# Layer 3's dense first block: the weights' relu on ACT, the addition and the mask in one DVE operation per head

## The chip, the cores and the metric

The kernel runs on one core of a Trainium2 chip. The metric is the device time of one execution in microseconds. The kernel before takes 1708.3 us, the median of three runs (1705.78 to 1711.26).

A core has five engines that run their own instruction queues in order: PE (matrix products), DVE (elementwise work and reductions), ACT (activations), POOL (here above all the issue of gathers) and SP (here the issue of plain loads and stores). They wait for each other through semaphores.

## The reference

Four graph layers run over 3327 nodes with 512 features and a sparse random adjacency `adj`, whose low-numbered nodes have many more edges than the others. After each layer the input is added and the rows are normalised. Only layer 3 is touched, a graph attention layer with four heads of 128 outputs:

```python
h = jnp.einsum('nf,hfo->hno', x, hamilton)
f_src = jnp.einsum('hno,ho->hn', h, a_src)
f_dst = jnp.einsum('hno,ho->hn', h, a_dst)
e = jax.nn.leaky_relu(f_src[:, :, None] + f_dst[:, None, :], ALPHA)
e = jnp.where((adj > 0)[None, :, :], e, NEG_INF)
attn = jax.nn.softmax(e, axis=-1)
h_prime = jnp.einsum('hnm,hmo->hno', attn, h)
out = jnp.transpose(h_prime, (1, 0, 2)).reshape(N, -1)
return jax.nn.elu(out)
```

## The kernel before

The nodes are cut into 26 blocks of 128 (the last has 127). Layer 3 first writes a table `t_d` to memory, one row per node, with the projected features of the four heads and their scores (520 floats a row). The sums over neighbours are then made in two ways.

**Blocks 1 to 25** use lists of edges. POOL gathers 128 table rows at a time (a chunk, L966) into a ring of 27 slots (22 in `gt`, 5 in `gx`). Groups of up to four chunks go through six stages, one stage per iteration of the main loop (`Gat.group`): 1, the gathers, and `far` on ACT (L1156); 2, `ds` on DVE (L1160); 3, small products `pg` on PE (L1168); 4, `sc` on DVE (L1178, L1179), two exponentials and `sel` on ACT (L1180, L1181, L1185); 5, the gathered rows times their weights on DVE (L1188); 6, the sums `acc` on PE (L1196), which give the ring's slots back.

**Block 0**, the heaviest, is done densely (`Gat.first_block`). Exponentials are factored so that the weight of neighbour j for node i and head h is `max(f1[i]*up[j], low[j])` times the 0/1 mask. `f1` is broadcast over the partitions once (`f1b`, L1102); `up` and `low` are made in `Gat.factors`. Each of the 26 blocks of neighbours is a unit (`unit(c)`):

- stage 1: SP loads 128 table rows into `gd` (L1119; four buffers, so unit c's load waits for the matmuls of unit c-4; for unit 25 it is 127 rows);
- stage 2: every fourth unit, ACT converts the mask of four units to `mk` (L1124; one buffer). DVE makes `wt` (two buffers), four L1128, one per head, and multiplies it with the mask, one L1130. ACT writes ones into a column of `gd` (L1131), for which the load must have landed;
- stage 3: PE adds the four heads' products to block 0's sums (L1134).

The order of all instructions on each engine is as the program writes them here; no scheduler moves them. `steps(n)` starts a unit and moves every live unit on by one stage, n times: 12 times before the first group, then twice in each iteration, ahead of the groups' stages. So in each iteration two units pass each stage, and then each live group does one of its own, older groups first. In the kernel before, PE's order from group 1's sums on is: unit 20, unit 21, group 1's sums, products of group 4, units 22 and 23, group 2's sums, products of group 5, unit 24, unit 25, group 3's sums, products of group 6, group 4's sums.

A block's end (`summed`, then L825) runs on ACT and DVE when its sums are complete.

Of the kernel before, what the change touches and what calls it, by code (L numbers as in the profile page):

```python
# [8 lines left out]
F32 = mybir.dt.float32  # L9
# [8 lines left out]
AF = mybir.ActivationFunctionType  # L18
ALU = mybir.AluOpType
# [4 lines left out]
P = 128  # L24
BIG = 1e30
EPS = 1e-5
GAT_ALPHA = 0.2
# [548 lines left out]
class Ring:  # L576
# [19 lines left out]
    def done(self):  # L596

        self.live.pop(0)
# [23 lines left out]
def sparse_path(ctx, tc, flag_i, x, adj, l0_w, l0_a1, l0_a2, l1_w_self, l1_b_self, l1_w_nb, l1_b_nb,  # L622
# [13 lines left out]
    nc = tc.nc  # L636
    N, D = x.shape
    NB = (N + P - 1) // P
# [10 lines left out]
    def pool_in(lay, name, bufs=1, **kw):  # L649
        return lay.enter_context(tc.tile_pool(name=name, bufs=bufs, reuse_waits="tile", **kw))  # L650
# [3 lines left out]
    keep = pool_in(ctx, "s_keep")  # L654
# [328 lines left out]
    class Gat:  # L983
        def __init__(self, name, table, H, OUT, w, k):
            self.table, self.H, self.OUT, self.w, self.k = table, H, OUT, w, k
            self.M = OUT + 2
            self.fall = keep.tile([P, 3 * H, NB], F32, name=name + "fall")
            self.own = keep.tile([P, 3, 2 * H, NB], BF16, name=name + "own")
            self.xsum = keep.tile([P, DC, NB], F32, name=name + "xsum")
            self.up, self.low = [keep.tile([P, H, NB], F32, name=name + x) for x in ("up", "low")] if k else (None,) * 2  # L990

        def products(self, ps, xt):

# [76 lines left out]
        def factors(self, pool, bc, f2):  # L1070

            H = self.H
            far = pool.tile([P, H], F32, name="farz")
            nc.vector.tensor_add(far, bc[:, :H], bc[:, 2 * H:3 * H])
            most = pool.tile([P, 4], F32, name="most")
            nc.vector.tensor_reduce(most[:, 0:1], far, AX.X, ALU.max)
            nc.vector.tensor_reduce(most[:, 1:3], bc[:, :2 * H].rearrange("p (s h) -> p s h", s=2), AX.X, ALU.max)
            nc.vector.tensor_reduce(most[:, 3:4], bc[:, 2 * H:], AX.X, ALU.max)  # L1080
            nc.vector.tensor_scalar(most[:, 0:1], most[:, 0:1], 0.0, 1.0 - GAT_ALPHA, ALU.max, ALU.mult)
            nc.vector.scalar_tensor_tensor(most[:, 0:1], most[:, 1:2], GAT_ALPHA, most[:, 0:1], ALU.mult, ALU.add)
            nc.vector.tensor_scalar(self.up, f2, most[:, 0:1], None, ALU.subtract)
            nc.vector.tensor_scalar(self.low, f2, GAT_ALPHA, most[:, 0:1], ALU.mult, ALU.subtract)
            for t in (self.up, self.low):
                nc.scalar.activation(t, t, AF.Exp)
            wide = pool.tile([P, 1], F32, name="wide")
            nc.vector.scalar_tensor_tensor(wide, most[:, 2:3], GAT_ALPHA, most[:, 0:1], ALU.mult, ALU.add)
            nc.vector.scalar_tensor_tensor(wide, most[:, 3:4], 1.0 - GAT_ALPHA, wide, ALU.mult, ALU.add)
            return wide  # L1090

        def first_block(self, pool, ps, pacc, mp, none, done):

            H, OUT, M = self.H, self.OUT, self.M
            hh = H // 2
            dg = pool.tile([P, H, P], F32, name="wt")
            for h in range(H):
                nc.vector.tensor_scalar(dg[:, h, :], ident, self.fall[:, h, 0:1], None, ALU.mult)
            pf = ps.tile([P, H * P], F32, name="pf", tag="pg")
            nc.tensor.matmul(pf, ones, dg.rearrange("p h i -> p (h i)"), start=True, stop=True)  # L1100
            f1 = pool.tile([P, H, P], F32, name="f1b", bufs=1)
            nc.scalar.activation(f1, pf.rearrange("p (h i) -> p h i", i=P), AF.Exp, scale=1.0 - GAT_ALPHA)  # L1102

            pl = ps.tile([P, H * P], F32, name="pl", tag="pg")
            nc.tensor.matmul(pl[0:1, :P], none, ident, start=True, stop=True)
            lone = pool.tile([P, H, P], F32, name="wt")[0:1, 0, :]
            nc.scalar.copy(lone, pl[0:1, :P])
            G = pool.tile([P, H, M], F32, name="gd", bufs=4)
            nc.sync.dma_start(G[0:1].rearrange("p h m -> p (h m)"), self.table[0:1, :])
            nc.scalar.copy(G[0:1, :, OUT], ones[0:1, :H])  # L1110
            acc = [pacc.tile([P, hh, M], F32, name="acc") for s in range(2)]
            for s in range(2):
                nc.tensor.matmul(acc[s], lone, G[0:1, s * hh:(s + 1) * hh, :], start=True, stop=False)
            masks = [None]

            def unit(c):
                m = LAST if c == NB - 1 else P
                G = pool.tile([P, H, M], F32, name="gd", bufs=4)
                nc.sync.dma_start(G[:m].rearrange("p h m -> p (h m)"), self.table[2 + c * P:2 + c * P + m, :])  # L1119
                yield  # L1120
                if c % 4 == 0:
                    masks[0] = mp.tile([P, 4, P], F32, name="mk")
                    n = min(4, NB - c)
                    nc.scalar.activation(masks[0][:, :n, :], row0[:, c:c + n, :], AF.Identity)  # L1124
                mask = masks[0]
                wt = pool.tile([P, H, P], F32, name="wt")
                for h in range(H):
                    nc.vector.tensor_scalar(wt[:m, h, :], f1[:m, h, :], self.up[:m, h, c:c + 1],  # L1128
                                            self.low[:m, h, c:c + 1], ALU.mult, ALU.max)
                nc.vector.tensor_mul(wt[:m], wt[:m], mask[:m, c % 4, None, :].to_broadcast([m, H, P]))  # L1130
                nc.scalar.copy(G[:m, :, OUT], ones[:m, :H])  # L1131
                yield
                for h in range(H):
                    nc.tensor.matmul(acc[h // hh][:, h % hh, :OUT + 1], wt[:m, h, :], G[:m, h, :OUT + 1],  # L1134
                                     start=False, stop=h % hh == hh - 1 and c == NB - 1)
                if c == NB - 1:
                    done(0, acc)

            for c in range(NB):
                yield unit(c)  # L1140
# [607 lines left out]
```

## Time and profile before

| what | value |
|---|---|
| median of three runs | 1708.3 us (1705.78 to 1711.26) |
| profiled execution, first to last instruction (span) | 1704.1 us |
| median less that span | 4.2 us |
| busy in the span: PE, DVE, POOL, ACT | 1523.7, 1243.4, 911.9, 773.2 us |
| four L1128 and one L1130, in the dense block | 28.2 + 17.2 us busy for 25 of 26 units |
| first L1128, last L1134 | 1381.6, 1449.5 us |

The page gives for the profiled execution the span from its first to its last instruction; a run's time is a few microseconds longer. Times inside the span count from its start. In the timeline and the chain the columns are start, duration, engine and line; a bracket gives the idle time before the instruction and what ended it. A matmul in fp32 is two instructions, so a unit's four heads appear as eight.

### The profile page before, as it was taken

Reading aid. Unit: us, or ns where it says so; the run is one execution under the profiler, and the core shown is the slowest. Engines: PE = TensorE matmul, PEld = TensorE weight load, DVE = VectorE, ACT = ScalarE, POOL = GpSimd, SP = SyncE. Lnnn points to the kernel's source line nnn. Section 1 sums busy time; section 2 is a strip of 40 time slices with the busy share of each in tenths; the row PEclk is TensorE's granted clock in tenths of the full one; section 3 lists DMA queues with packets and bytes.
Section 4 is the critical chain, followed back from the end, with each engine's and each line's share of the span. In section 5 each row is a group of like instructions: output and inputs, shape, how many; then the busy total and the mean of one; then the engine's idle time right before and its main releaser. Section 6 shows DMA issues by size and latency. Waiting matters only on the chain.

```text
span 1704.1 us, 25362 instructions
## 1 busy us (share of the span) xinstructions
PE 1523.7 (89%) x7947; PEld 981.5 (58%) x7947; DVE 1243.4 (73%) x3256; ACT 773.2 (45%) x2411; POOL 911.9 (54%) x1008
## 2 busy tenths in 40 slices
PE   5798958999999999999999999889989866998774
PEld 4565746777666664444444444446555545877653
DVE  8999988999998973124777884565434468798986
ACT  6557855667776764111111121122223222566664
POOL 2000067777666613646776552477777552677770
PEclk9999979999999999999999999999999987999997
DMA  8623687998775637978998776589999664677772
GB/s 300 233 100 107 207 288 237 313 309 266 258 231 176 179 90 282 317 237 272 341 328 296 246 241 241 204 279 317 318 312 322 234 227 157 189 230 224 227 220 74
DMA packets 121982, 410.17 MB, mean 241 GB/s; under 512 B 24768, under 2 KB 26304, under 8 KB 121838
## 3 DMA queue, kind: packets, MB, share of 16 engines
q0 software_dynamic: 69584, 286.13, 52.8%
q1 hardware_dynamic: 52254, 122.32, 20.4%
q8 instruction: 65, 1.06, 0.3%
q14 instruction: 79, 0.65, 0.1%
HBM read 360.34 MB, written 48.04 MB: 240 GB/s over the span
## 4 chain that ended last, share of the span: by engine, by line
PE 61%; DVE 16%; DMA 11%; ACT 6%; issue 3%; POOL 2%; SPq 0%; DVEq 0%; ACTq 0%; POOLq 0%
PE po L765 20%; PE acc L1196 15%; PE acc L1474 14%; DMA gt<-t_d,idx 7%; PE po L998 6%; PE pt L750 2%; DVE cand L877 2%; DVE gt L1188 2%; DMA gx<-t_d,idx 2%; POOL gt L966 2%; PE pg L1168 2%; DMA gd<-t_d 1%; DVE cand L891 1%; DVE sl L889 1%; ACT h L1213 1%
## 5 line engine op out<-in xcount | busy, mean ns | idle before, releaser
L966 POOL DMA_INDIRECT gt<-t_d,idx x739 | 742.1, 1004 | 578.9 <-DVE some L893 210.6
L1196 PE MATMUL acc<-gt,sel 128*128 128x264 f32 (+4 forms) x1656 | 413.7, 399 | 27.1 <-issue 20.1
L1196 PEld LDWEIGHTS acc<-gt,sel 128*128 128x128 f32 (+2 forms) x1656 | 311.4, 195 | 97.8 <-issue 42.9
L1188 DVE TENSOR_TENSOR gt<-gt,pg 128x1536 f32<-128x1536 f32 (+2 forms) x128 | 238.6, 1864 | 6.3 <-ACT gt L1181 2.9
L765 PE MATMUL po<-wn,xt 128*128 128x512 f32 x416 | 192.9, 607 | 3.8 <-ACT xt L753 3.8
L1474 PE MATMUL acc<-gt,sall 128*128 128x512 bf16 x489 | 117.3, 379 | 17.6 <-DMA gt<-t_d,idx 14.3
L765 PEld LDWEIGHTS po<-wn,xt 128*128 128x128 f32 x416 | 77.2, 193 | 89.4 <-issue 78.4
L966 POOL DMA_INDIRECT gx<-t_d,idx x107 | 107.6, 1006 | 38.6 <-issue 14.9
L877 DVE MAX8 cand<-val 128x8 f32<-128x832 uint16 (+38 forms) x259 | 125.7, 522 | 0.0
L1474 PEld LDWEIGHTS <-sall 128*128 128x128 fp8e4 x603 | 58.3, 97 | 98.4 <-issue 35.3
L1474 PE MATMUL acc<-gt,sel 128*128 128x512 bf16 (+3 forms) x486 | 113.3, 379 | 0.0
L998 PE MATMUL po<-gt,xt 128*128 128x268 f32 x416 | 106.0, 400 | 2.0 <-ACT xt L757 1.7
L1474 PEld LDWEIGHTS <-sel 128*128 128x128 bf16 (+3 forms) x603 | 57.9, 98 | 80.0 <-issue 22.7
L1156 ACT ACTIVATE far<-place,nmid 128x384 int16<-128x384 int16 (+3 forms) x137 | 86.9, 637 | 37.5 <-DVE ds L1160 34.5
L753 ACT COPY xt<-pt 128x512 f32<-128x512 f32 x86 | 50.8, 591 | 113.3 <-PE pt L750 113.2
L998 PE MATMUL po<-w,xt 128*128 128x262 f32 x416 | 96.2, 384 | 1.6 <-ACT xt L757 1.6
L765 PE MATMUL po<-wl,xt 128*128 128x512 f32 x208 | 94.0, 594 | 2.9 <-ACT xt L753 2.9
L765 PE MATMUL po<-wx,xt 128*128 128x512 f32 x208 | 94.3, 596 | 1.3 <-ACT xt L753 1.2
L750 PE MATMUL pt<-s_ident,xres 128*128 128x128 f32 x520 | 79.9, 277 | 17.4 <-DMA xres<-in_x_dram 16.6
L750 PEld LDWEIGHTS pt<-s_ident,xres 128*128 128x128 f32 x520 | 63.8, 143 | 46.2 <-issue 31.2
L1009 ACT COPY tg<-po 128x264 f32<-128x264 f32 (+1 forms) x104 | 39.9, 392 | 110.8 <-PE po L998 108.9
L849 ACT ACTIVATE m<-ab 128x1664 bf16<-128x1664 int32 x50 | 80.4, 1607 | 20.5 <-DMA ab<-in_adj_dram 15.6
(273 smaller groups left out, 2555.4 us busy)
## 6 DMA issues: line engine op xcount, KB each, us to landing
ab<-in_adj_dram SPq DMA_DIRECT2D x25, 832.0 KB
ab<-in_adj_dram SPq DMA_DIRECT2D x25, 831.5 KB
t_d<-t SPq DMA_DIRECT2D x50, 384.0 KB
gt<-t_d POOLq DMA_DIRECT2D x38, 384.0 KB, 7.8
gt<-t_d,idx POOLq DMA_INDIRECT x739, 4.8
t_d<-tg SPq DMA_DIRECT2D x25, 264.0 KB
t_d<-tg SPq DMA_DIRECT2D x25, 260.0 KB
gd<-t_d SPq DMA_DIRECT2D x25, 260.0 KB
```

What stands on the lines that cost most here:

```text
L750: nc.tensor.transpose(pt[:, c, :], src[:, c * P:(c + 1) * P], ident)
L753: nc.scalar.copy(xt, pt)
L765: nc.tensor.matmul(po, xt[:, c, :], w[:, c], start=c == 0, stop=c == DC - 1)
L849: nc.scalar.activation(m, ab[s], AF.Sign, accum_out=half[:, s, b:b + 1])
L877: nc.vector.max(out=top, in_=seg)
L966: nc.gpsimd.indirect_dma_start(out=t[:m, c, :], out_offset=None, in_=table[:, :], in_offset=bass.IndirectOffsetOnAxis(ap=l.idx[:m, c0 + c: ...
L998: nc.tensor.matmul(pw[s], xt[:, c, :], self.w[:, c, s, :], start=c == 0, stop=c == DC - 1)
L1009: nc.scalar.copy(tb[:, s * hh:(s + 1) * hh, :], by_head[:, :, 1:])
L1156: nc.scalar.activation(far[:, :g * P], place[:, c0 * P:(c0 + g) * P], AF.Abs, bias=l.nmid, scale=2.0)
L1188: nc.vector.tensor_mul(Gc[:, :, :OUT], Gc[:, :, :OUT], w[:, :g].rearrange("p c (h o) -> p (c h) o", o=1).to_broadcast([P, g * H, OUT]))
L1196: nc.tensor.matmul(accs[b][s], S[:m, c, :], G[:m, c, s * hh * M:(s + 1) * hh * M], start=at + c == 0, stop=at + c == chunks_of[b] - 1)
L1474: nc.tensor.matmul(accs[b], S[:m, c, :], G[:m, c, k * D:(k + 1) * D], start=at + c + k == 0, stop=k == 2 and at + c == n - 1)
```

## The change

`low` is kept negated (`nlow`), by one more DVE operation in `factors`. Per head, ACT computes `relu(f1*up + nlow)`; a stage later, DVE computes `(that - nlow) * mask` in one operation per head. The result is the same, since `max(a, b) = relu(a - b) + b`. The unit has four stages rather than three: load; `mk` and relu; DVE's operations and the ones copy; matmuls.

```diff
-            self.up, self.low = [keep.tile([P, H, NB], F32, name=name + x) for x in ("up", "low")] if k else (None,) * 2
+            self.up, self.nlow = [keep.tile([P, H, NB], F32, name=name + x) for x in ("up", "nlow")] if k else (None,) * 2
...
-            nc.vector.tensor_scalar(self.low, f2, GAT_ALPHA, most[:, 0:1], ALU.mult, ALU.subtract)
-            for t in (self.up, self.low):
+            nc.vector.tensor_scalar(self.nlow, f2, GAT_ALPHA, most[:, 0:1], ALU.mult, ALU.subtract)
+            for t in (self.up, self.nlow):
                 nc.scalar.activation(t, t, AF.Exp)
+            nc.vector.tensor_scalar(self.nlow, self.nlow, -1.0, None, ALU.mult)
...
                 for h in range(H):
-                    nc.vector.tensor_scalar(wt[:m, h, :], f1[:m, h, :], self.up[:m, h, c:c + 1],
-                                            self.low[:m, h, c:c + 1], ALU.mult, ALU.max)
-                nc.vector.tensor_mul(wt[:m], wt[:m], mask[:m, c % 4, None, :].to_broadcast([m, H, P]))
+                    nc.scalar.activation(wt[:m, h, :], f1[:m, h, :], AF.Relu, bias=self.nlow[:m, h, c:c + 1],
+                                         scale=self.up[:m, h, c:c + 1])
+                yield
+                for h in range(H):
+                    nc.vector.scalar_tensor_tensor(wt[:m, h, :], wt[:m, h, :], self.nlow[:m, h, c:c + 1],
+                                                   mask[:m, c % 4, :], ALU.subtract, ALU.mult)
                 nc.scalar.copy(G[:m, :, OUT], ones[:m, :H])
                 yield
```

In PE's order each unit's matmuls move back by one unit: unit 19, unit 20, group 1's sums, products of group 4, units 21 and 22, group 2's sums, products of group 5, units 23 and 24, group 3's sums, products of group 6, unit 25, group 4's sums. On ACT, the relu of unit c+1 stands behind the ones copy of unit c. The other engines' orders are otherwise unchanged.

## The prediction

> **What bounds the kernel now.** I read the page first, then the chain that ended last in order of time around the changed lines (1376 to 1460 us), then POOL's instructions one by one, then the groups by shape for prices. The chain, from the stretch of layer 3's dense block:
>
> ```profile
> 1404.23 1.12 DVE wt L1128 x4
> 1405.45 0.69 DVE wt L1130
> ...
> 1426.57 0.61 ACT far L1156
> 1427.32 2.10 PE acc L1134 x8
> 1429.47 18.04 DMA gd<-t_d
> 1447.85 2.09 PE acc L1134 x8
> 1449.93 5.49 PE acc L1196 x16
> ...
> 1455.64 3.60 PE acc L1196 x16
> ```
>
> To 1422 the chain runs on DVE: four L1128 and one L1130 per unit, 1.75 us from one unit to the next. Then it changes. Unit 21's matmuls (1427.32) free the buffer that unit 25's load needs; that load takes 18.04 us, unit 25's matmuls wait for it, and only behind them on PE stand group 3's sums (L1196, 1449.93) and group 4's (1455.64). The last load, not DVE, is what the chain holds here.
>
> POOL's instructions say what this costs at the end:
>
> ```profile
> 1431.89 0.95 POOL L966 DMA_INDIRECT gt<-t_d,idx  x1 [22.90 <-ACT pg L1180]
> ...
> 1452.41 0.96 POOL L966 DMA_INDIRECT gt<-t_d,idx  x1 [9.47 <-issue]
> ...
> 1457.47 0.95 POOL L966 DMA_INDIRECT gt<-t_d,idx  x1 [0.30 <-issue]
> ...
> 1665.51 0.94 POOL L966 DMA_INDIRECT gt<-t_d,idx  x1 [0.30 <-issue]
> ```
>
> POOL fills the ring by 1409 and stands 22.90 us until group 1's sums give slots back, then 9.47 us until group 3's do. From 1452.41 to its last gather at 1665.51 no gap exceeds 0.31 us: one gather each 1.26 us, 38 us before the end. So the end moves with the time at which POOL becomes free for good. A microsecond of DVE saved in the dense block is worth something only if it brings that forward.
>
> Prices of the operations (groups by shape: busy us, mean ns of one):
>
> ```profile
> L1128 DVE TENSOR_SCALAR wt<-f1b,g3up,g3low 128x128 f32<-128x128 f32 x100 | 28.2, 355 | 6.5 <-PE acc L1134 3.2 <-ACT f1b L1102 2.9 <-PE acc L1113 0.4
> L1130 DVE TENSOR_TENSOR wt<-wt,mk 128x512 f32<-128x512 f32 x25 | 17.2, 688 | 1.3
> ...
> L1213 ACT ACTIVATE h<-acc,rden 128x128 f32<-128x128 f32 x104 | 29.0, 357 | 0.0
> L825 ACT ACTIVATE o<-e,nm,rs 128x512 f32<-128x512 f32 x26 | 20.8, 801 | 2.8 <-DVE nm L824 2.8
> L1218 DVE SCALAR_TENSOR_TENSOR h<-h,xres 128x512 f32<-128x512 f32 x26 | 18.0, 691 | 12.7 <-ACT e L1216 12.5
> L1216 ACT ACTIVATE e<-h 128x512 f32<-128x512 f32 x26 | 16.4, 630 | 0.8
> ```
>
> L825 has two per-partition operands (bias and scale) as the new relu has; L1216 has none, and at the same shape is 0.17 us shorter. L1213 has one, at the relu's own shape.
>
> [...]630 ns without, 801 with two, and the chain shows L825 as 0.71, which is 0.09 less.[...]L1218's 691 ns beside L1130's 688 says it costs like a two-tensor one.[...]unit 25's, the only one with 127 rows, takes 18.04 us, the 128-row ones 3.3 to 6.3 from issue to their ACT copy.
>
> **The change, part by part.**
>
> *Removed from DVE:* per unit 4 L1128 and one L1130, 1.75 us.
>
> *Added to DVE:* per unit four scalar_tensor_tensor of 128x128. [...]From one to the next about 0.21 (neighbours on this engine overlap by 0.08, as L1130 does), up to 0.29. Four: 0.84 to 1.16 us, so DVE is relieved by 0.6 to 0.9 us a unit. It can't use it: each of the four waits for its head's relu.
>
> *Added to ACT:* per unit four relus. [...]from one to the next 0.48 - 0.09 = 0.39; four occupy 1.56 us. Bounds: 0.26 each if they went like L1213 (one operand, four in 1.03 to 1.12), 0.48 without overlap. I take 0.39. With the ones copy (0.10) and a quarter of mk (0.53, plus some 0.3 in which it now waits for DVE's reading of the old mk), a unit is 1.56 + 0.10 + 0.2 = 1.86 us of ACT. That is as long as DVE's 1.75 was. And ACT also has, in each pair of units from group 1 on, far (0.62), two exponentials (0.24) and sel (0.53). ACT takes over as the pacing engine.
>
> *New waits on ACT.* The ones copy of unit c waits for its load, and relu c+1 is queued behind it; formerly DVE worked ahead there. Behind relu stand far, the exponentials and sel of the groups. In turn relu c waits for unit c-2's matmuls (two wt buffers). The last ones copy still stands in front of group 5's exponentials, as before.
>
> *The extra DVE negation in the factors:* it waits for ACT's second Exp (ends 1374.56; DVE's next operation started 1374.15) and takes 0.2: DVE's chain to L1098, PE's broadcast and f1b all shift by 0.65 us. No cover: PE waits 6.22 us there for DVE.
>
> *Moved:* a unit has one stage more, so its matmuls come a half iteration later in program order: PE does units 0 to 20 before group 1's sums (formerly 0 to 21), and unit 21 comes after them and after group 4's small products; unit 25 comes after group 3's sums and before group 4's. SP's loads keep their order, but unit 25's load still waits for unit 21, now behind group 1.
>
> *The sum.* ACT from its first relu at 1382.9 (1381.52 + 0.65 for f1b, mk 0.6) to unit 20's ones copy: 21 x 1.56 = 32.8 for relu, 21 x 0.10 = 2.1 for ones, 5 x 0.8 = 4.0 for mk with its wait, 5 far 3.1, two groups' exponentials and sel 1.5, zero copies 0.3: 43.8, so 1426.7. ACT also waits, for loads in the stretch where the gathers keep the DMA engines full and about 2 us for group 2's scores, which stand behind the 2.28 us L1188 on DVE: 1429. Unit 20's matmuls at half clock, 2.1: group 1's sums start about 1431.7, against 1429.20: **+2.5**.
> Unit 21 then ends after those sums (5.7 at half clock, as before), the products (0.5) and its own 1.1: 1439.0, against 1429.44 (+9.5). The load lands 18.04 later, 1457.0; ones 0.2 and unit 25 at half clock 2.1[...]: group 4's sums start at 1459.3 against 1455.64. That is 9.5 less the 5.7 of group 3's sums and products, which no longer stand between: **+3.7**.
> POOL: in the kernel before, the first slot came back 2.5 us after group 3's sums began (1449.93 to 1452.41, half clock) and 1.3 after group 2's (1436.94 to 1438.25, full clock). The gather at 1457.47 becomes 1459.3 + 1.3 to 2.5 = 1460.6 to 1461.8: +3.1 to +4.3. It is the thirteenth after the ring filled, in both; from there POOL is saturated.
> The profiled span becomes 1704.1 + 4 = 1708.1. The median of the runs lies 4.2 above that span, and I let that offset stand: 1708.3 + 4 = **1712.3 us**.
>
> **Rivals.**
> - *ACT follows the rate of L1213* (0.26 from relu to relu). 21 x 4 x 0.13 = 11 us less ACT work, of which the waits for loads and for wt give back most; group 1's sums start about 1.6 us before 1429.20. By the sum above group 4's sums are then level with before (-4.1 + 3.7), and if PE also keeps full clock through units 20, 21 and group 1 (1.0 + 1.0 + 2.1), up to 4.5 us earlier, 6 with the first slot's release. For it: four L1213 in 1.03. Against it: L825's 801 ns. 1702 to 1708.5; say 1706.
> - *Slower by more than 0.3%: relu to relu 0.48, or PE's half clock lasts longer.* Place: from group 1's sums to group 4's. PE was at half clock for unit 21 (2.10 rather than 1.13) and group 1 (5.72 rather than 3.6) behind a 2.9 us pause; the change makes the pauses before unit 20 as long and the one before unit 25 some 7 us (6.0 before). If every PE step between 1428 and 1462 is at half clock, unit 21 and 22 add 1, group 2's and 3's sums delay nothing, group 4's add 2. With no overlap on ACT, 21 x 4 x 0.09 = 7.6 us are added directly. It decides once group 1's sums start 4 us late or more (1433.2). 1714 to 1718; say 1716.
> - *The shift is absorbed:* POOL's saturation, or the 38 us of tail on ACT and DVE, has slack. Speaks against it: no POOL gap over 0.31 in 213 us, and the chain at the end leaves POOL only at 1665.51, for that gather's landing. 1708.3.
> - *The change doesn't do what it says:* no; relu(f1*up - low) + low is max(f1*up, low), DVE does lose the 4+1 operations, only the time isn't worth what it looks like.
>
> **How the numbers follow.** +4 case 0.46 (range 1709 to 1714.5); slower rival 0.36; fast ACT 0.12; absorbed 0.06. 0.3% is 5.1 us, about what a measurement of this kernel tells from no change (the three runs span 5.5): the +4 case lies inside it, save a sixth of it. Slower: 0.36 less 0.02, plus 0.08 = 0.42. Faster, that is below 1703.2: a third of the fast-ACT case, 0.04. The rest, 0.54, is within. Range: 1705 leaves out the fastest end, 1718 the worst half-clock and no-overlap ends.
>
> **What the profile after would show.** Right: relus of 0.48 us and 0.39 apart; DVE idle on ACT between its four operations; units 1.9 to 2.1 us apart; group 1's sums near 1431.7; group 3's sums ahead of unit 25; unit 25's load issued near 1439 and 18 us long; POOL's final run from a gather near 1461. Wrong: relus 0.26 apart and group 1 before 1429 (first rival), group 1 after 1433 (second), or POOL's last gather later but the end not (third). If POOL has further gaps after 1462, the step from group 4 to the end fails.

## The result and the profile after

The changed kernel takes 1712.89 us (median of 20 runs, 1707.96 to 1715.24); the kernel before took 1708.53 us beside it (20 runs, 1705.19 to 1714.2). The ratio is 1.0023, 95% interval [1.0015, 1.0031]: 4.4 us slower, by less than 0.3% save for the upper end of the interval. The predicted 1712.3 us lies 0.6 us from it.

The chain that ended last in the kernel after, in order of time (start, duration, what):

```profile
1394.40 1.63 ACT wt L1129 x4
...
1416.43 1.56 ACT wt L1129 x4
...
1425.88 1.56 ACT wt L1129 x4
...
1427.72 2.28 DVE gt L1192
...
1430.66 0.60 issue
...
1432.42 2.09 PE acc L1138 x8
1434.51 4.24 PE acc L1200 x16
...
1439.05 1.00 PE acc L1138 x8
...
1440.11 18.77 DMA gd<-t_d
...
1459.20 2.09 PE acc L1138 x8
1461.28 4.50 PE acc L1200 x16
```

Where the chain of before ran through DVE's four L1128 and one L1130 it now runs through ACT's relus. From the first relu (1386.20) to unit 20's ones copy (1432.19) ACT stands idle for 2.9 us in all: it has become the pacing engine. The end of the stretch has the same shape as before with its parts exchanged: unit 20's matmuls (1432.42), group 1's sums (1434.51), only then unit 21 (1439.05), whose end lets unit 25's load start (1440.11); that load is 18.77 us long, and behind unit 25 stand group 4's sums (1461.28).

POOL's instructions in the kernel after where it had to wait, with the idle time before each in the bracket:

```profile
1436.86 1.02 POOL L966 DMA_INDIRECT gt<-t_d,idx  x1 [24.49 <-DVE sc L1183]
...
1442.56 0.95 POOL L966 DMA_INDIRECT gt<-t_d,idx  x1 [0.90 <-ACT mk L1125]
...
1449.08 0.97 POOL L966 DMA_INDIRECT gt<-t_d,idx  x1 [1.83 <-issue]
...
1463.76 0.95 POOL L966 DMA_INDIRECT gt<-t_d,idx  x1 [9.94 <-ACT far L1160]
...
1672.27 0.92 POOL L966 DMA_INDIRECT gt<-t_d,idx  x1 [0.30 <-issue]
```

The two long stands (POOL waiting for a free slot of the ring) are still there, 24.49 us (22.90 before) and 9.94 us (9.47). The engine named in a bracket is inferred and need not be the one that frees a slot: the long stands end 2.35 and 2.48 us after the start of the sums on PE that give slots back, group 1's (1434.51) and group 4's (1461.28). After 1463.76 no gap between gathers is longer than 0.31 us, and the last gather starts at 1672.27.

The groups by shape (busy us, mean ns of one, idle time before it and what ended it), kernel after:

```profile
L1129 ACT ACTIVATE wt<-f1b,g3nlow,g3up 128x128 f32<-128x128 f32 x100 | 41.0, 481 | 3.4 <-PE acc L1138 3.2
L1133 DVE SCALAR_TENSOR_TENSOR wt<-wt,g3nlow,mk 128x128 f32<-128x128 f32 x100 | 33.6, 346 | 19.2 <-ACT wt L1129 16.2
```

A relu takes 481 ns, and four in a row 1.63 us, so 0.38 to 0.39 from one to the next. DVE waits 16.2 us for relus in this block.

Times of two executions can't be set side by side as they stand. The two profiled executions differ ahead of the change, as the small matmul `pb` (L1043) shows, up to which both execute the same work. Its start before, and then after:

```profile
1372.23 0.39 PE L1043 MATMUL pb<-dgm,s_ones 16*128 16x16 f32 x2 [0.63 <-DVE dgm L1041]
```

```profile
1375.62 0.39 PE L1043 MATMUL pb<-dgm,s_ones 16*128 16x16 f32 x2 [0.63 <-DVE dgm L1041]
```

Those 3.39 us aren't the change's: in the profiles of e1 to e4 below, `pb` starts anywhere from 1370.62 to 1376.20. So from here on positions are counted from `pb`:

| from `pb`, us | before | after | difference |
|---|---|---|---|
| group 1's sums start | 56.97 | 58.68 | +1.7 |
| unit 21's matmuls end | 57.2 | 64.4 | +7.2 |
| unit 25's matmuls start | 75.62 | 83.58 | +8.0 |
| group 4's sums start | 83.26 | 85.46 | +2.2 |
| thirteenth gather after the ring filled | 85.24 | 88.14 | +2.9 |
| last gather | 293.28 | 296.65 | +3.4 |
| end of the span | 331.87 | 335.08 | +3.2 |

The thirteenth gather is the first of POOL's unbroken run in the kernel after; in the kernel before that run starts four gathers earlier (1452.41).

### The profile page after: what moved, and what is told of

It is laid out like the page before. It is cut to its first block, busy times and chain, and to the rows that moved or that the text cites. A ratio compares the mean times of both kernels' runs of the same rounds, so it can differ in the third digit from the quotient of the medians.

```text
span 1710.7 us, 25381 instructions
## 1 busy us (share of the span) xinstructions
PE 1532.7 (90%) x7900; PEld 990.9 (58%) x7947; DVE 1232.7 (72%) x3231; ACT 813.6 (48%) x2515; POOL 914.3 (53%) x1008
## 4 chain that ended last, share of the span: by engine, by line
PE 40%; DMA 10%; ACT 6%; DVE 5%; issue 3%; POOL 1%; DVEq 0%; ACTq 0%; POOLq 0%; SPq 0%
PE po L765 15%; PE acc L1478 12%; DMA gt<-t_d,idx 8%; PE acc L1200 7%; PE po L998 4%; PE pt L750 2%; ACT wt L1129 1%; DMA gx<-t_d,idx 1%; DVE gt L1192 1%; DMA gd<-t_d 1%; ACT h L1217 1%; DVE st L770 1%; PE acc L1138 1%; DVE e L1223 1%; DVE h L1222 1%
## 5 line engine op out<-in xcount | busy, mean ns | idle before, releaser
L998 PE MATMUL po<-gt,xt 128*128 128x268 f32 x416 | 111.3, 415 | 2.9 <-ACT xt L757 1.8
L1478 PE MATMUL acc<-gt,sel 128*128 128x512 bf16 (+2 forms) x472 | 112.6, 379 | 0.7
L998 PEld LDWEIGHTS po<-gt,xt 128*128 128x128 f32 x416 | 79.5, 201 | 22.5 <-issue 5.0
```

What stands on the lines that cost most here:

```text
L998: nc.tensor.matmul(pw[s], xt[:, c, :], self.w[:, c, s, :], start=c == 0, stop=c == DC - 1)
L1478: nc.tensor.matmul(accs[b], S[:m, c, :], G[:m, c, k * D:(k + 1) * D], start=at + c + k == 0, stop=k == 2 and at + c == n - 1)
```

## The experiments

The theory under test is the prediction's: the dense block matters through the time at which POOL becomes free for good. The change is two changes, an engine (DVE's operations partly to ACT) and a stage (matmuls one unit later), and the last transfer, of 127 rows, stands between them and that time. Rivals: the stage does the harm; the load is innocent; the relu's price is hidden by the loads. The first four experiments ran on one chip, where the kernel before took 1708.01 us (49 runs). The later ones ran on two other chips, where every kernel took longer: the kernel before 1909.42 us (22 runs) beside e5, e7, e8 and e9 on the second chip, and 1904.72 us (51 runs) beside e10 to e13 on the third. Of those only ratios and differences beside each other are used.

**e1: relu on ACT, three stages.** The changed kernel without its added stage:

```diff
...
                                          scale=self.up[:m, h, c:c + 1])
-                yield
                 for h in range(H):
...
```

> The changed kernel without the added stage: relu, DVE's operations and the ones copy in one stage, so unit 21's matmuls stand ahead of group 1's sums again and unit 25's ahead of group 3's. Theory A (ACT's two-operand relus set the pace, and the moved stage gives as much as it takes): unit 25's load is issued some 2 us earlier than in the changed kernel, but group 3's sums wait behind unit 25 again, so POOL's unbroken run of gathers is not earlier; 1713 to 1717, that is 0 to 4 us over the changed kernel. Theory B (the loss comes from moving the matmuls one stage back, which puts the last load behind group 1's sums): the move's cost is given back and the time falls to 1708 to 1709, that of the kernel before.

Measured: 1715.24 us, ratio 1.0050 [1.0037, 1.0063]. PE's timeline of e1 (start, duration, engine, line; idle time before it in the bracket):

```profile
1437.36 2.09 PE L1137 MATMUL acc<-gd,wt 128*128 128x129 f32 x8 [4.31 <-ACT gd L1134]
1439.24 4.80 PE L1199 MATMUL acc<-gt,sel 128*128 128x260 f32 x16
...
1457.58 2.09 PE L1137 MATMUL acc<-gd,wt 127*128 127x129 f32 x8 [6.63 <-ACT gd L1134]
```

With `pb` at 1376.20, group 1's sums start at 63.04, 6.1 us later than before. So the engine alone costs more than the whole change, and the stage gives some back; the time lies in theory A's range and far from B's.

**e2: DVE's operations of before, four stages.** The other half of the change alone, in the kernel before:

```diff
                 nc.vector.tensor_mul(wt[:m], wt[:m], mask[:m, c % 4, None, :].to_broadcast([m, H, P]))
                 nc.scalar.copy(G[:m, :, OUT], ones[:m, :H])
                 yield
+                yield
```

> The kernel before with DVE's old five operations, but with the matmuls one stage later, as in the changed kernel. Theory A: DVE paces as before; group 1's sums stand behind one unit less (about 4 us earlier by the order), unit 25's load is issued some 3 us later because unit 21 now stands behind those sums, and group 3's sums no longer wait for it; POOL's last run starts 1 to 3 us earlier than before: 1705.5 to 1708. Theory B: the later load costs 4 us by itself: 1712 to 1713.

Measured: 1704.45 us, ratio 0.9987 [0.9979, 0.9994], a little below theory A's range; the stage by itself is a gain. PE's timeline of e2:

```profile
1422.98 4.59 PE L1197 MATMUL acc<-gt,sel 128*128 128x260 f32 x16 [0.48 <-DVE gt L1189]
...
1449.23 2.09 PE L1135 MATMUL acc<-gd,wt 127*128 127x129 f32 x8 [9.66 <-ACT gd L1131]
1451.11 5.78 PE L1197 MATMUL acc<-gt,sel 128*128 128x260 f32 x16
```

One unit fewer stands before group 1's sums (`pb` at 1370.62, so 52.36, 4.6 us earlier than before), which returns POOL's slots earlier; unit 25 then waits 9.66 us for its load, but stands behind group 3's sums rather than ahead of them.

Together e1 and e2 split the change. Differences from the kernel before, positions from `pb`:

| | group 1's sums | group 4's sums | last gather | end of the span | median, us |
|---|---|---|---|---|---|
| relu, three stages (e1) | +6.1 | +5.0 | +5.5 | +5.4 | +7.2 |
| DVE, four stages (e2) | -4.6 | -2.8 | -1.9 | -0.7 | -3.6 |
| sum of the two | +1.5 | +2.2 | +3.7 | +4.7 | +3.7 |
| both: the changed kernel | +1.7 | +2.2 | +3.4 | +3.2 | +4.4 |

Up to the last gather the parts add up to within 0.3 us, in the medians to 0.7; at the end of the span they are 1.5 apart, since e2's stretch after its last gather is 1.2 us longer than that of the kernel before. The engine costs some 5 us at group 4's sums and the stage returns 2.8 there. What is added after that isn't explained by these traces.

**e3 and e4: unit 25's load in two parts.** The changed kernel (e3) and the kernel before (e4), with the cut into 112 and 15 rows that `rows_of` makes for other loads of the last block. Nothing else changes; the first 25 loads stay one transfer each.

```diff
-                nc.sync.dma_start(G[:m].rearrange("p h m -> p (h m)"), self.table[2 + c * P:2 + c * P + m, :])
+                for p0, p1 in rows_of(c):
+                    nc.sync.dma_start(G[p0:p1].rearrange("p h m -> p (h m)"),
+                                      self.table[2 + c * P + p0:2 + c * P + p1, :])
```

> The changed kernel with unit 25's load of 127 rows issued as two loads of 112 and 15 rows. Theory A (unit 25's long load is the link between the dense block and POOL's last run): the load takes 4 to 6 us rather than 18.8, group 4's sums follow group 3's without the 8 us stop, POOL's last run starts 8 to 9 us earlier, and the time falls by as much, to 1704 to 1705.5. Rival C (ACT's pace alone sets the loss and the long load is hidden or its wait is taken over by something behind it): within 2 us of 1712.9.

> The kernel before with the same split of the last load. Theory A: the 6 us stop ahead of unit 25 goes, group 3's sums come 6 to 7 us earlier, and so does POOL's last run: 1701 to 1702.5, some 2 to 3 us better than the changed kernel with the split, which is what ACT's pace costs without the long load. Rival C: within 2 us of 1708.5.

Measured: e3 1702.09 us, ratio 0.9967 [0.9957, 0.9976]; e4 1702.2 us, ratio 0.9965 [0.9955, 0.9975]. PE's timeline of e3:

```profile
1447.59 3.67 PE L1202 MATMUL acc<-gt,sel 128*128 128x260 f32 x16
...
1451.34 1.14 PE L1140 MATMUL acc<-gd,wt 127*128 127x129 f32 x8
1452.32 3.67 PE L1202 MATMUL acc<-gt,sel 128*128 128x260 f32 x16
```

And POOL's gaps in e3 above half a microsecond, after the ring was full:

```profile
1436.45 0.95 POOL L966 DMA_INDIRECT gt<-t_d,idx  x1 [25.12 <-DVE sc L1185]
...
1442.86 0.95 POOL L966 DMA_INDIRECT gt<-t_d,idx  x1 [1.68 <-ACT mk L1127]
...
1449.38 0.96 POOL L966 DMA_INDIRECT gt<-t_d,idx  x1 [1.84 <-issue]
```

Unit 25 follows group 3's sums without a pause and at 1.14 us rather than 2.09, and POOL's second stand, 9.94 us, is gone altogether. Group 4's sums start at 77.71 after `pb` (85.46 in the changed kernel), the last gather at 288.62 (296.65). The load is over after at most 7.6 us (its parts are issued at 1440.41 and 1440.8, and the ones copy on ACT, which needs both, starts at 1448.00), against 18.77. The trace shows that the parts land sooner, not why. The last gather comes 8.0 us earlier, as theory A had it. From median to median the gain is larger than expected, 10.8 us; what the rest comes from isn't shown.

In e4 unit 25 starts 0.93 us after PE came free:

```profile
1444.34 1.13 PE L1136 MATMUL acc<-gd,wt 127*128 127x129 f32 x8 [0.93 <-ACT gd L1133]
```

Group 4's sums start at 73.72, and the last gather is 8.2 us earlier than in the kernel before. An advantage of DVE's form of 2 to 3 us once the long load is gone was expected, and it is open: in the two traces the last gather is 3.5 us ahead of e3's (285.11 against 288.62), but the medians are equal to 0.1 us, and their difference is uncertain by some 2 us.

**e5 and e10, e11: the price of the relu's operands.** e5 and e11 are the same kernel, the changed one with a relu that has neither scale nor bias; block 0's weights are not those of the reference, so it stands for time alone. e10 is the changed kernel again, for a neighbour on the same chip.

```diff
-                    nc.scalar.activation(wt[:m, h, :], f1[:m, h, :], AF.Relu, bias=self.nlow[:m, h, c:c + 1],
-                                         scale=self.up[:m, h, c:c + 1])
+                    nc.scalar.activation(wt[:m, h, :], f1[:m, h, :], AF.Relu)
```

> The changed kernel with the relu's bias and scale left out (so block 0's weights are not the reference's); four stages, orders and all else as they are. Theory A (ACT's two-operand relus set the pace of the dense block): a relu takes about 0.30 us and the next starts 0.21 later, so ACT has some 0.7 us less a unit; the units then go at the pace of the loads, group 1's sums start 4 to 6 us earlier counted from the start of the dense block; unit 25's load is issued 3 to 5 us earlier, still takes 18 to 19, and POOL's last run starts about 3 us earlier: 1709 to 1711. Rival D (loads, DVE or PE's clock set the pace, ACT only waits for them): group 1's sums within 1.5 us of where they were, 1712 to 1714.

Measured: ratio 0.997 [0.9951, 0.9989]. The direction was expected, the size was larger than either theory allowed. The changed kernel had not run on that chip. Both therefore ran side by side on the third:

> The changed kernel itself, a second time, so that the next three stand beside it on one chip. Theory A: the ratio to the kernel before is what it was, 1.0015 to 1.0031 on a chip where the kernel before takes about 1708 us. If all transfers are slower on this chip, the ratio can differ by some 0.2%: the loads then hide a part of ACT's time.

> The changed kernel with a relu without scale and bias (about 0.30 us in place of 0.48, so four in 0.9 instead of 1.6). Theory F: the fourth stage by itself is a gain (0.9987 on DVE), and what the change loses is the price of the relu's two operands; without them the ratio falls to 0.997 to 0.9995, 5 to 9 us under the changed kernel. Theory B: unit 25's load, still some 18 us behind unit 21, keeps all but 1 to 3 us of it: 1.0003 to 1.0018.

Measured: e10 1909.81 us, ratio 1.0019 [0.9998, 1.0041]; e11 1901.0 us, ratio 0.9991 [0.9973, 1.001]. The relu in e10, by shape, and then in e11:

```profile
L1129 ACT ACTIVATE wt<-f1b,g3nlow,g3up 128x128 f32<-128x128 f32 x100 | 41.0, 481 | 20.7 <-remote 11.2 <-PE acc L1138 9.4
```

```profile
L1129 ACT ACTIVATE wt<-f1b 128x128 f32<-128x128 f32 x100 | 22.5, 296 | 28.7 <-PE acc L1137 10.6 <-issue 10.5 <-remote 7.6
```

The chains of the two, first e10 and then e11, where unit 20, group 1, unit 25 and group 4 stand:

```profile
1572.38 2.09 PE acc L1138 x8
1574.47 5.28 PE acc L1200 x16
...
1582.76 17.64 DMA gd<-t_d
...
1600.73 2.09 PE acc L1138 x8
1602.82 4.76 PE acc L1200 x16
```

```profile
1570.11 2.09 PE acc L1137 x8
1572.20 5.53 PE acc L1199 x16
...
1580.41 18.17 DMA gd<-t_d
...
1598.90 2.09 PE acc L1137 x8
1600.99 4.79 PE acc L1199 x16
```

With `pb` at 1500.89 in e10 and 1504.50 in e11, group 1's sums start 5.9 us earlier without the operands, group 4's 5.4 us, the last gather 5.1 us (1850.18 and 1848.67); the medians differ by 8.8 us. The load is as long in both, so it doesn't hide the relu: it starts earlier. The 5 us are what moving to ACT cost in e1 against before, and in the changed kernel against e2 (85.46 less 80.49 at group 4's sums). So theory F holds as far as this chip tells, though the intervals of e10 and e11 overlap a little and each includes 1 (set beside each other, the means of their 22 and 14 runs differ by 6.2 us, uncertain by some 3.7): the loss of the change is the price of a relu with two operands. The 0.185 us of it per relu is 18.5 us of ACT in 100 relus, of which a bit more than a quarter reaches group 4. On this chip ACT also stands idle for 20.7 us ahead of its relus (3.4 in the profile further up), so the share need not be the same where it waits less.

**e7: four stages and the split load together, on DVE.** The kernel before with e2's and e4's edits.

> The kernel before with both edits that gained: DVE's old five operations, matmuls one stage later, and unit 25's load split into 112 and 15 rows. Theory A: in the four-stage kernel the long load still held group 4's sums by 9.7 us; without it they follow group 3's, and both gains add: POOL's last run 9 to 10 us earlier than in the kernel before, 1698 to 1700.5. Rival: the two edits remove the same wait, and the time stays at the 1702 of the split load alone.

Measured: ratio 0.9936 [0.9912, 0.996]. The two gains, 0.13% and 0.35% on the first chip, seem to add: the 0.9965 of the split alone, which the rival expected, lies just outside the interval. But that figure is the first chip's, neither edit ran alone on this one, and there are only seven runs.

**e8, e12 and e9, e13: one unit per group.** The split load, and units dealt out more evenly: three before the first group and one per iteration, with DVE's form of before (e8, e12 are one kernel) and with the relu (e9, e13 are one kernel).

```diff
-DENSE0 = 12
-DENSE = 2
+DENSE0 = 3
+DENSE = 1
```

> The kernel before with the split load, three units instead of twelve ahead of the first group, and one unit instead of two per iteration. Theory A (the end moves with POOL's idle time in the dense block, 22.9 us before group 1's sums and what follows): group 1's sums then come before or soon after the ring is full; DVE needs about 1.75 + 3.05 = 4.8 us an iteration against POOL's 5.03 for four gathers, so POOL is nearly saturated from the start and loses at most some 8 us of its former 32: 1680 to 1692. Rival E (ACT's and DVE's work at the blocks' ends, not POOL, becomes the bound, since DVE has no slack left): less than 8 us better than the split load alone, 1695 to 1702.

> The changed kernel with the same three edits (split load, three units ahead, one unit per iteration). Theory A: as for the kernel before with them; with one unit an iteration ACT has about 1.86 + 1.5 us of dense and group work an iteration, far from its limit, and DVE 0.8 to 1.4 + 3.05, so here the change relieves the engine with the least slack: 1677 to 1692, and not slower than the kernel before with the same edits, at best 3 us faster. Rival: ACT's longer queue delays the groups' exponentials, and it is 2 us or more slower than that kernel.

> DVE's form of before, unit 25's load in two parts, one unit per group from the start. Theory A: 0.983 to 0.990, as on the other chip; 1680 to 1691 us where the kernel before takes 1708. Theory E: there the transfers were slower and the early return of slots was worth more; here no more than the split load alone, 0.996 or above.

> The changed kernel with the split load and one unit per group. Theory G: spread over the groups, ACT's four relus (1.56 us) stand ahead of a group's exponentials, sel and h, and cost 0.2 to 0.5% against the same order with DVE's form: 0.987 to 0.994. Theory H: with one unit per group neither engine is the bound and the two are equal within 0.15%.

Measured: e8 0.9861 [0.9842, 0.988], e9 0.9903 [0.9885, 0.992]; the second time e12 0.9928 [0.9902, 0.9953], e13 0.994 [0.9921, 0.9958]. All four are faster than the kernel before. The first pair lies in theory A's range; e12 lies between its two theories, above A's 0.983 to 0.990 and below E's 0.996. The split is in all four and wasn't run alone on these chips, so the ratios don't say how much is due to dealing the units out. POOL's stands over 4 us in e12 behind the full ring:

```profile
1551.27 0.95 POOL L966 DMA_INDIRECT gt<-t_d,idx  x1 [10.02 <-PE acc L1198]
...
1585.23 0.95 POOL L966 DMA_INDIRECT gt<-t_d,idx  x1 [5.96 <-PE acc L1198]
...
1635.65 0.95 POOL L966 DMA_INDIRECT gx<-t_d,idx  x1 [4.76 <-PE acc L1198]
...
1674.47 0.95 POOL L966 DMA_INDIRECT gt<-t_d,idx  x1 [4.32 <-PE acc L1198]
```

The long wait for group 1 is 10.02 us, and 9.15 with the relu (e13); in e10, the relu on the same chip with the old dealing, it is 38.29. Group 1's sums no longer stand behind 20 units. Whether the relu is worse than DVE's form in this order is open. By e8 and e9 it is 0.4% slower, against e9's theory A, but these have six runs each, and e8's reach from 1880.99 to 1901.03 us; by e12 and e13 it is 0.1% (medians 1889.4 and 1891.08), as theory H has it, with intervals that overlap for the most part. And e12 differs from e8, the same kernel on another chip, by 0.7%. In the traces ACT's queue does hold PE longer with the relu, as theory G says; e12 first, then e13, PE's timeline at the first wait for `h` (an operation on ACT at a block's end):

```profile
1582.86 5.57 PE L1198 MATMUL acc<-gt,sel 128*128 128x260 f32 x12 [5.34 <-ACT h L1215]
```

```profile
1590.60 5.00 PE L1202 MATMUL acc<-gt,sel 128*128 128x260 f32 x12 [7.58 <-ACT h L1219]
```

None of it reaches the last gather: that starts 330.95 us after `pb` in e12 and 330.99 in e13 (330.91 in e8, 331.44 in e9). The rest of the difference arises after it, where the two take 51.08 and 52.72 us; but that stretch varies with DVE's form too (50.47 in e8, 53.07 in e7). Neither form was run on the first chip, so what the best version, DVE with one unit per group, gives there isn't known; on the other two it gained 0.5 to 1.6% by the two intervals.

## Why the prediction was right

- *ACT's price.* 0.48 us a relu and 0.39 apart were predicted, 481 ns and 1.63 for four measured. The 0.48 was L825's 801 ns less some 320 for 384 elements, and the trace of before shows 315 to 322 for that many: `far` (L1156) takes 717 ns for 512 elements and 402 for 128, `sel` (L1185) 614 for 512 and 399 for 256. The relu added no load of a function table: ACT has four in either trace, the last at 1376.73 before and 1380.69 after, ahead of the first relu. Units were to be 1.86 us apart by ACT's own work and 1.9 to 2.1 in all: four of them take 7.7 us (the two copies of the mask at 1393.86 and 1401.55), 1.92 each, and the twenty from the first relu (1386.20) to unit 20's (1428.37) 2.1 each. Right, as was preferring L825's price to L1213's rate.
- *ACT's waits.* From the first relu to unit 20's ones copy 46.1 us were predicted and 46.0 measured, but not from these parts. The 2.3 us for loads and group 2's scores are in truth 0.4 for the scores, none for a load (though the DMA share is 0.92 from 1385 to 1409, and 0.95 before), and 0.9 for earlier units' matmuls; ACT's other work took some 1 us more. That the total fits is luck.
- *DVE can't use its relief.* Right: it waits 16.2 us for relus. Its single operation was mis-sized: 346 ns where 0.29 us was put down. That was L1218's 691 ns less 400 for 384 elements, the step that L1188 shows in the trace of before (674 ns for 512 elements, 1207 for 1024); from L1218 to the new operation the measured difference is 345. In e11, where ACT doesn't hold it back, four take 1.12 to 1.13 us, near the predicted upper end of 1.16. So the relief is about L1130's 0.7 us.
- *Factors.* +0.65 predicted, +0.59 measured (from `pb` to `pf`).
- *Group 1's sums +2.5.* Measured +1.7. Most of the difference is a slip in the sum: 1429 and 2.1 make 1431.1, not 1431.7, and that is +1.9. The absolute mark of 1433, past which the slower rival was to hold, was passed (1434.30), and yet the rival did not hold: 3.39 of it had come from upstream. The mark should have been given as a distance from a point that the change doesn't reach.
- *Unit 21 ends +9.5.* Measured +7.2, as group 1's sums stood +1.7, not +2.5, and took 4.44 us, not the 5.72 of before. The term "5.7 at half clock, as before" is the one mis-sized: such sums of 16 matmuls take 3.67 us at full clock (granted clock 1.00 for group 2's, 1437 to 1440.5, before), and group 1's behind a unit at half clock took 4.24 (e4) to 5.74 (e11). In the kernel before, PE's granted clock is 0.50 for 6.0 us from unit 21's start, and single matmuls of group 1 then go from 641 to 382 ns; in the kernel after it is 0.50 for only 3.4 us from unit 20's start. So in these traces the length of the slow stretch is a range and not a constant; what sets it isn't shown.
- *Load 18.04, unit 25 at half clock.* 18.77 and 2.09 (granted clock 0.50): right, and the load 0.7 longer. PE's pause ahead of it was to be some 7 us and is 8.01. In the traces of before, after, e1 to e4, e10 and e11 every unit from unit 20 on behind a pause of 2.87 us (unit 21 before) to 9.66 (unit 25 in e2) took 2.09, against 1.13 to 1.16 at full clock; but in the kernel after one took 2.09 behind a pause of only 0.87 (1425.93), so that the pause is the reason isn't shown.
- *Group 4 +3.7.* Measured +2.2. Both smaller terms above enter here, less the longer load.
- *POOL +3.1 to +4.3, then saturated.* +2.9, just under the low end. No gap over 0.31 us followed. The last gather is +3.4, the span's end +3.2 and the medians +4.4: the shift isn't absorbed, so that rival falls.
- *The offset of 4.2 us from span to median.* Wrong as a length: a run takes 1.7 us more than its span (1712.43 for the profiled 1710.7; 2.1 to 2.2 in e2's and e7's runs). The profiled execution of before was simply a short one, about 1705.8 by the same 1.7. The term did its work only because it was carried over as a difference to the median.

What the prediction did not separate is that its two halves have opposite signs. It booked the stage as a cost at unit 21 and then got its return back as "no longer stand between"; the experiments show it as a gain of 2.8 us at group 4 and the engine as a loss of 5.0. The sum was nearly right without the parts being known. So the mechanism was right, and so was the sign: ACT paces, the last load passes the delay on, and POOL carries it to the end. That the number came within 0.6 us is in part luck: the shift at group 4 was to be 3.7 and was 2.2, the profiled pair ends 3.2 apart, and what brings the medians to 4.4 has no term in the prediction.

## What to carry to other kernels

Work taken from one engine to another paid here only by what the new engine's queue then released: 0.7 us of DVE per unit was bought with 1.6 us of ACT, and the chain followed it. Look for the thing behind the wait that ends last before the engines: one transfer of 127 rows, cut in two, was worth 6 us in the kernel before and 11 in the changed one by the medians, and 8 in each by the last gather, while moving work from DVE to ACT gained nothing in any order tried. And measure positions from a point that the change doesn't reach, since two executions that do the same work up to there can be 3 us apart at it.

## What the runs showed of the hardware

The same program took 11% longer on another chip with DVE, ACT and POOL no busier. Engines' busy times in the changed kernel's page, first from its run further up and then from e10:

```profile
PE 1532.7 (90%) x7900; PEld 990.9 (58%) x7947; DVE 1232.7 (72%) x3231; ACT 813.6 (48%) x2515; POOL 914.3 (53%) x1008
```

```profile
PE 1585.0 (83%) x7900; PEld 1014.3 (53%) x7947; DVE 1233.2 (65%) x3231; ACT 813.8 (43%) x2515; POOL 906.2 (48%) x1008
```

The spans are 1710.7 and 1901.3 us, but DVE, ACT and POOL are busy for the same time; PE, whose clock was granted at 0.963 and 0.927 on average, for 52 us more. The difference begins where gathers run. A table by stretch (us from the span's start; length; busy time and number of instructions of PE, PE's weight loads, DVE, ACT and POOL; granted clock, DMA share, GB/s), changed kernel and then e10:

```profile
100.00:200.00 100.00, 91.20 (x507) 63.96 (x506) 95.99 (x361) 67.59 (x245) 0.00 (x0) 0.97 0.34 113
300.00:400.00 100.00, 98.92 (x692) 75.13 (x691) 96.25 (x232) 65.54 (x178) 74.48 (x78) 1.00 0.90 296
```

```profile
100.00:200.00 100.00, 90.43 (x530) 64.77 (x529) 96.84 (x365) 69.67 (x241) 0.00 (x0) 0.98 0.35 116
300.00:400.00 100.00, 85.28 (x560) 61.84 (x558) 81.36 (x190) 56.43 (x146) 57.70 (x59) 0.98 0.73 237
```

In the first of these stretches POOL has nothing to do, and the two are level; in the second, with gathers, POOL does 59 instructions in 100 us instead of 78, at 237 instead of 296 GB/s. From the last long stand to the last gather the same gathers take 244.9 us (1605.30 to 1850.18) instead of 208.5, so there POOL isn't saturated in the final run. What slows the gathers is open; no run was made for it. Ratios of kernels in which gathers set the pace should therefore be taken on one chip.
